# Two attention layers in one kernel: VectorE and ScalarE in a planned order, PSUM banks by turns, scores six units ahead

## The chip, the cores and the metric

One core of a Trainium2 chip. The metric is the device time of the whole kernel in microseconds; lower is better.

## The reference

Two layers over images of 512 channels and 32 x 32 = 1024 tokens, eight images. The first quantises q, k and v to 255 levels with one scale each, taken over all images, and has 8 heads of 64 channels; the second has one head of 512 channels. Both end in a projection that is added to their input.

```python
def _L0_conv_ref(x, gn_w, gn_b, qkv_w, qkv_b, proj_w, proj_b):
    xf = x.reshape(b, c, T)
    h = group_norm(xf, gn_w, gn_b)
    qkv = jnp.einsum('oc,bct->bot', qkv_w, h) + qkv_b[None, :, None]
    q, k, v = jnp.split(qkv.reshape(b * NUM_HEADS, -1, T), 3, axis=1)
    q, k, v = fake_quant(q), fake_quant(k), fake_quant(v)
    w = jnp.einsum('bct,bcs->bts', q * scale, k * scale)
    w = jax.nn.softmax(w, axis=-1)
    a = jnp.einsum('bts,bcs->bct', w, v).reshape(b, c, T)
    return xf + jnp.einsum('oc,bct->bot', proj_w, a) + proj_b[None, :, None]

def _L1_conv_ref(x, gn_w, gn_b, wq, bq, wk, bk, wv, bv, wp, bp):
    t = group_norm(x, gn_w, gn_b).reshape(B, C, H * W).transpose(0, 2, 1)
    q, k, v = (t @ w.T + b for w, b in ((wq, bq), (wk, bk), (wv, bv)))
    attn = jax.nn.softmax(q @ k.transpose(0, 2, 1) / sqrt(C), axis=-1)
    proj = (attn @ v) @ wp.T + bp
    return x + proj.transpose(0, 2, 1).reshape(B, C, H, W)
```

## The kernel before

The kernel runs in four stretches of time.

The first computes q, k and v of layer 0 for all images (tiles `qkps`, `vps`), writes them to DRAM and gathers the extrema for the scales. The second folds the weights of layer 1 (`fold`) while it does layer 0's attention for image 0. The third is the long one: for each image it runs layer 1 (`layer1`) and, between the pieces of it, layer 0's attention for the next image. The fourth is layer 1 of the last image, with nothing between.

Layer 0's attention is cut into units (`attention`): a unit is one block of 128 keys for two heads and 512 queries, 64 units per image. `scores` forms `st` on TensorE, ScalarE takes the exponential into `pt` (L770), and `pt` is split into two halves of 16 bits, `two`: a cast (L777, on ScalarE for even units and on GpSimd for odd ones; on VectorE while the flag `alone` holds, in the second stretch) and a subtraction on VectorE (L778). `weighted` then forms `av` (values) and `sm` (sums over keys). A generator step (`advance`) does four units, a block; scores are formed four units ahead of `weighted`. `finish` copies `av` and `sm` on ScalarE at the end of eight units (L815, L816), sends the sums over DRAM to be inverted, and VectorE divides (L832).

Layer 1 is made of products of matrices, each done as a group of seven products of half size (`seven`): `a_block` (tile `g`), `v_block2` (`v2ps`), `s_block` (`s`, the scores) and `o_run` (`o`), ten groups per image. One group uses two PSUM banks, x and y, into which products are accumulated; between products ScalarE copies a part out (`keep`, tiles `kept_u`, L1055, L1092, L1188), VectorE adds a kept part to a bank (`add`, L1068, L1110, L1125, L1159), and one result is taken whole. In the last image a third bank is used (`third`). A product of g, v2ps or s is four matmuls of 256 columns, one of o eight. `project` is layer 0's last projection (tile `pj`, evicted into `h` at L922), `norm1` the norm of layer 1. In `o_run` the sums over keys (`acc`, L1293) are totalled by TensorE (`sm_l`) and inverted over DRAM (`inverse1`).

TensorE's order is written out by hand: `mm` (L105) ties each matmul to the one before. VectorE and ScalarE have no such tie; the framework's scheduler places their instructions. Pieces that aren't urgent are put into a list (`later`) and taken out one at a time by `chore`, after a count of steps, or all of a name by `settle`. Loads of x1, wp0, wm and h are issued from ScalarE's queue, the others from SP's.

Of the kernel before, what the change touches and what calls it, by code (L numbers as in the profile page):

```python
# [17 lines left out]
P = 128  # L18
# [35 lines left out]
def attn_pair_kernel(  # L54
# [11 lines left out]

    x_v = x.rearrange("b (cc p) h w -> b p cc (h w)", p=P)
# [8 lines left out]
    nc.scalar.dma_start(vec, vecs)  # L76
    ones = const.tile([P, P], F32, name="ones")
    nc.vector.memset(ones, 1.0)
# [10 lines left out]
    nc.vector.memset(gavg, 0.0)  # L89
    with tc.tile_pool(name="band", bufs=1) as band:  # L90
        low = band.tile([P, 32], F32, name="low")
        nc.vector.memset(low[:, 0:GS], 1.0)
        nc.vector.memset(low[:, GS:32], 0.0)
        low_t = band.tile([P, 32], F32, name="low_t")
        nc.vector.transpose(low_t, low)
        for r in range(0, P, 32):
            sq = slice(r, r + 32)
            nc.vector.tensor_tensor(gavg[sq, sq], low[sq, :], low_t[sq, :], ALU.is_equal)
    nc.vector.tensor_scalar(gavg, gavg, 1.0 / GS, None, ALU.mult)
    ident = const.tile([P, P], F32, name="ident")  # L100
    make_identity(nc, ident)
# [3 lines left out]
    def mm(*args, **kw):  # L105
        ins = nc.tensor.matmul(*args, **kw).ins  # L106
# [10 lines left out]
    def aggregate(mv, st, i):  # L117
        nc.vector.bn_aggr(mv[:, i, :], st[:, i, :, :].rearrange("p a s -> p (a s)"))


    def norm_steps(
        src, dst, wcol, bank, nm, ccs=range(CC), fine=False, put=lambda hf, work: work(), mv=None
# [4 lines left out]
        n, c0 = len(ccs), ccs[0]  # L127
        if mv is None:
            st, mv = stat_tiles(n, nm)
            for i, cc in enumerate(ccs):  # L130
                for hf in range(NH):
                    nc.vector.bn_stats(st[:, i, hf, :], src(cc, hf))
# [8 lines left out]
        nc.vector.tensor_sub(d, mv[:, :, 0], ps)  # L141
        mean = small.tile([P, n], F32, tag=f"gmean{n}", name=f"gmean_{nm}")
        nc.vector.tensor_copy(mean, ps)
        nc.vector.tensor_mul(d, d, d)
        nc.vector.tensor_add(d, d, mv[:, :, 1])
# [4 lines left out]
        nc.vector.tensor_scalar(rstd, ps2, EPS, None, ALU.add)  # L150
        nc.gpsimd.tensor_tensor(rstd, rstd, mhalf[:, 0:n], ALU.pow)
        nc.vector.tensor_mul(rstd, rstd, vec[:, wcol + c0 : wcol + c0 + n])
        for hf in range(NH):
            for i, cc in enumerate(ccs):
                put(hf, lambda i=i, cc=cc, hf=hf: nc.vector.tensor_scalar(  # L155
# [27 lines left out]
    with ExitStack() as fast:  # L183
# [50 lines left out]
        def weigh(bank, room, w, wide, nm):  # L234
# [9 lines left out]
            nc.scalar.copy(room, ps)  # L244
# [17 lines left out]
        def widen(dst, col):  # L262
            for e in range(CC):
                nc.vector.tensor_scalar(
# [3 lines left out]
        with tc.tile_pool(name="p1w", bufs=1) as p1w, tc.tile_pool(name="p1", bufs=3) as p1, tc.tile_pool(  # L268
# [15 lines left out]
            def load_folded(tag, ij):  # L284

                two = l1p.tile([P, 2, CC, C], F32, tag=tag, name=f"wn_{tag}")
                for n, i in enumerate(ij):
                    wn[i] = two[:, n]
                    nc.scalar.dma_start(wn[i], w_sq[i])
# [33 lines left out]
            def weight_sums():  # L323
                tt = nc.vector.tensor_tensor
# [28 lines left out]
            def token_sums(b):  # L353
# [4 lines left out]
                tt = nc.vector.tensor_tensor  # L358
# [13 lines left out]
            def add_max(dst, ps, other, mx):  # L372
                nc.vector.tensor_tensor_reduce(
# [1457 lines left out]
```

## Time and profile before

| | us |
|---|---|
| median of 3 runs | 2813.78 (2807.37 to 2815.15) |
| the profiled execution | 2814.92, its span 2813.1 |
| TensorE busy (PE) | 2621.5, 93% |
| VectorE busy (DVE) | 1924.6, 68% |
| ScalarE busy (ACT) | 1152.1, 41% |
| GpSimd busy (POOL) | 280.9, 10% |
| mean granted TensorE clock | 0.990 |

Busy time is the time in which at least one instruction of the engine was under way, and its share is one over the whole span; it has to be read by stretches, which have different limits. In the profile a line such as L106 is a helper's, so tile names tell more than lines. A row of waits names the waiting engine, its tile and line, and after the arrow what released it.

### The profile page before, as it was taken

The numbers are of one execution on the slowest core, as the hardware profiler recorded it, in microseconds if no ns is written. First come the engines' busy times: TensorE is split into PE (matmuls) and PEld (weight loads), VectorE is DVE, ScalarE is ACT, GpSimd is POOL, SyncE is SP. The second block draws the span as 40 slices with busy tenths as digits, with TensorE's granted clock in tenths as the row PEclk, the third lists the DMA queues.
The fourth block names the chain that finished last, engine by engine and source line by source line (L and its number), as shares of the span: only waits on it lengthen the run. The fifth ranks groups of instructions, "written<-read, shape, count | busy, mean of one in ns | idle before, by whom it ended". The sixth has DMA issues, their size and how long they took to land.

```text
span 2813.1 us, 33256 instructions
## 1 busy us (share of the span) xinstructions
PE 2621.5 (93%) x13110; PEld 1650.1 (59%) x13110; DVE 1924.6 (68%) x2772; ACT 1152.1 (41%) x1474; POOL 280.9 (10%) x248
## 2 busy tenths in 40 slices
PE   7999999997779999999999999999999999999998
PEld 3455555552226665665566566656665665567687
DVE  6766665668987767776776677677767766764534
ACT  0011111117955563645465455535563645463021
POOL 0000000000011111111111111111111111110000
PEclk9999999999999999999999999999999999999999
DMA  5233322333321223123212421241233123201401
GB/s 195 101 120 120 113 112 90 120 118 122 106 87 31 72 85 107 54 72 117 76 39 64 128 72 39 85 131 44 73 92 98 52 72 113 71 10 46 142 8 43
DMA packets 147461, 241.94 MB, mean 86 GB/s; under 512 B 26592, under 2 KB 92128, under 8 KB 145760
## 3 DMA queue, kind: packets, MB, share of 16 engines
q1 hardware_dynamic: 116448, 181.50, 19.5%
q10 hardware_dynamic: 30848, 58.23, 6.3%
q8 instruction: 104, 1.70, 0.3%
q14 instruction: 61, 0.50, 0.1%
HBM read 152.86 MB, written 86.28 MB: 85 GB/s over the span
## 4 chain that ended last, share of the span: by engine, by line
PE 50%; DVE 22%; issue 11%; ACT 10%; DMA 5%; POOL 1%; ACTq 0%; SPq 0%; DVEq 0%; POOLq 0%
PE s L106 10%; PE qkps L106 10%; DVE two L778 9%; PE o L106 7%; ACT pt L770 5%; PE pj L106 5%; PE vps L106 5%; PE v2ps L106 4%; PE g L106 4%; ACT two L777 3%; PE av L106 3%; DMA rs<-rs_d 2%; PE st L106 2%; PE sm L106 1%; DVE ao L832 1%
## 5 line engine op out<-in xcount | busy, mean ns | idle before, releaser
L778 DVE TENSOR_TENSOR two<-pt,two 128x1024 f16<-128x1024 f32 x512 | 617.1, 1236 | 254.8 <-ACT two L777 240.4
L770 ACT ACTIVATE pt<-st,esc 128x1024 f32<-128x1024 f32 x512 | 554.7, 1124 | 214.9 <-PE st L106 168.8
L777 POOL CAST two<-pt 128x1024 f16<-128x1024 f32 x218 | 260.9, 1197 | 1537.5 <-ACT pt L770 1531.7
L777 ACT CAST two<-pt 128x1024 f16<-128x1024 f32 x256 | 270.0, 1055 | 1.1
L106 PE MATMUL av<-two,v 128*64 128x512 f16 x2048 | 255.9, 388 | 0.3
L398 ACT ACTIVATE u<-qkps,qkb 128x512 f32<-128x512 f32 x84 | 57.7, 687 | 476.5 <-PE qkps L106 472.1
L106 PE MATMUL s<-g,h 128*128 128x256 f32 x1024 | 238.2, 382 | 13.7 <-DVE p L1125 10.1
L106 PE MATMUL pj<-ao,wp 128*128 128x512 f32 x512 | 223.0, 594 | 0.0
L106 PEld LDWEIGHTS s<-g,h 128*128 128x128 f32 x1024 | 191.7, 190 | 51.1 <-DVE p L1125 16.6
L106 PE MATMUL st<-q,k 64*128 64x512 bf16 x1024 | 166.1, 386 | 56.6 <-ACT pt L770 44.1
L106 PE MATMUL s<-g,sums 128*128 128x256 f32 x768 | 183.7, 386 | 14.3 <-ACT kept_u L1092 14.3
L106 PEld LDWEIGHTS <-v 128*64 128x64 f16 x2048 | 104.5, 110 | 134.4 <-issue 62.5
L106 PE MATMUL o<-p,v 128*128 128x256 f32 x768 | 174.1, 382 | 0.0
L106 PEld LDWEIGHTS s<-g,sums 128*128 128x128 f32 x768 | 142.0, 190 | 50.0 <-ACT kept_u L1092 22.7
L106 PE MATMUL qkps<-x,wqkv 128*128 128x512 f32 x352 | 165.4, 613 | 2.2 <-DVE x L155 2.2
L106 PEld LDWEIGHTS pj<-ao,wp 128*128 128x128 f32 x512 | 96.6, 190 | 119.0 <-issue 115.2
L106 PEld LDWEIGHTS o<-p,v 128*128 128x128 f32 x768 | 144.2, 190 | 27.2 <-issue 8.5
L106 PE MATMUL g<-h,wa 128*128 128x256 f32 x512 | 127.8, 394 | 30.7 <-DVE kept_u L1159 14.4
L106 PE MATMUL qkps<-sums,wa 128*128 128x512 f32 x336 | 153.3, 592 | 0.0
L106 PE MATMUL sm<-two,ones 128*32 128x512 f16 x2048 | 141.2, 387 | 0.0
L106 PEld LDWEIGHTS <-k 64*128 64x128 bf16 x1024 | 35.2, 94 | 174.3 <-issue 173.7
L106 PE MATMUL v2ps<-wm,h 128*128 128x256 f32 x512 | 121.9, 385 | 10.9 <-DVE v L1110 6.6
(218 smaller groups left out, 3530.6 us busy)
## 6 DMA issues: line engine op xcount, KB each, us to landing
rs<-rs_d SPq DMA_DIRECT2D x80, 256.0 KB
x<-in_x_dram SPq DMA_DIRECT2D x32, 512.0 KB
raw<-q_d SPq DMA_DIRECT2D x32, 512.0 KB
raw<-k_d SPq DMA_DIRECT2D x32, 512.0 KB
raw<-v_d SPq DMA_DIRECT2D x32, 512.0 KB
x_d<-h SPq DMA_DIRECT2D x64, 256.0 KB
x<-x_d ACTq DMA_DIRECT2D x64, 256.0 KB
out_dram<-x SPq DMA_DIRECT2D x64, 256.0 KB
```

Source lines behind the costliest of these rows:

```text
L106: ins = nc.tensor.matmul(*args, **kw).ins
L398: nc.scalar.activation(dst, x, AF.Identity, bias=bias)
L770: nc.scalar.activation(pt, st, AF.Exp, scale=esc)
L777: cast(two[:, 0], pt)
L778: nc.vector.tensor_tensor(two[:, 1], pt, two[:, 0], ALU.subtract)
L832: nc.vector.scalar_tensor_tensor(aot, aot, scl[:, 2:3], rs, ALU.mult, ALU.mult)
```

## The change

A recording layer, `InOrder`, stands in front of VectorE and ScalarE. From the third stretch on it ties every instruction of an engine to the one before, as `mm` does for TensorE. It keeps a clock per engine: `mm` advances TensorE's by the number of columns, `do` places an urgent piece with its duration, and `later` lists a piece with its duration, the time from which it can run, and one by which it should. `fill` puts listed pieces ahead of an urgent one as far as they fit before it can begin.

```diff
+    class InOrder:
+        planned = False
+        def __getattr__(self, name):
+            op = getattr(self.engine, name)
+            def call(*args, **kw):
+                ins = op(*args, **kw).ins
+                if InOrder.planned:
+                    if self.last is not None:
+                        tc.add_manual_dep(ins, self.last.name, IN_ORDER, reason="order")
+                    self.last = ins
+            return call
+        def do(self, cost, work, ready=None):
+            if InOrder.planned:
+                ready = pe.t + 0.25 if ready is None else ready
+                self.fill(ready)
+                self.t = max(self.t, ready) + cost
+            work()
+            return self.t
+        def later(self, name, cost, work, ready=0.0, within=30.0):
+            if InOrder.planned:
+                self.chores.append((name, cost, work, max(ready, pe.t), pe.t + within))
+            else:
+                work()
+        def fill(self, limit):
+            if self is dve:
+                act.fill(limit)
+            while True:
+                best, names = None, set()
+                for i, (name, cost, _, ready, due) in enumerate(self.chores):
+                    if name in names:
+                        continue
+                    names.add(name)
+                    begin = max(self.t, ready)
+                    if begin + cost > limit + 0.15:
+                        continue
+                    key = (begin, due)
+                    if best is None or key < best[0]:
+                        best = key, i
+                if best is None:
+                    return
+                self.begin(best[1])
+    dve, act, pe = InOrder(nc.vector), InOrder(nc.scalar), InOrder(nc.tensor)
+    def elements(n):
+        return 0.1 + n * 1.06e-3
+    def awaits(t):
+        pe.t = max(pe.t, t + 0.1)
```

In `mm` `pe.t += math.prod(rhs.shape[1:]) * 1.677e-3 * part` is added. All instructions of VectorE and ScalarE are now issued through `dve` and `act`.

In `attention` all casts that fall into the planned part are ScalarE's, scores are formed six to ten units ahead, and `pt` has four buffers instead of three:

```diff
-        ptp = fast.enter_context(tc.tile_pool(name="ptp", bufs=3))
+        ptp = fast.enter_context(tc.tile_pool(name="ptp", bufs=4))
...
-                cast = nc.scalar.copy
-                if s % 2:
-                    cast = nc.vector.tensor_copy if alone else nc.gpsimd.tensor_copy
...
+                def cast():
+                    at_hand.add(u)
+                    act.copy(two[:, 0], pt)
+                    dve.later("sum", elements(1024), rest, act.t + 0.1, 9.0)
+                if InOrder.planned or s % 2 == 0:
+                    act.later("cast", 1.02, cast, there, 7.0)
+                else:
+                    dve.tensor_copy(two[:, 0], pt)
+                    rest()
...
-                    scores(u + 4)
-                    scores(u + 5)
-                weighted((u, u + 1) if dense else range(u, u + 4))
+                two(scores, u + 6)
...
+                    over_keys(range(u, u + 4))
+                    totals(range(u, u + 4))
+                    two(split, u + 6)
+                    two(scores, u + 8)
+                if s == NT - 4:
+                    finish(b, j, hf)
+                two(split, u + 8)
```

In `seven` the order of the products and of what is taken out changes, and the third bank goes. `free` and `turn` follow the banks in the plan:

```diff
-            product(0, x, True)
-            keep(0, x)
-            product(1, y, True)
-            add(0, y)
-            product(2, x, False)
-            keep(1, x)
-            product(3, y, True)
-            product(4, x, False)
-            keep(2, x)
-            add(2, y)
-            if third is None:
-                product(5, x, False)
-                whole(x)
-            else:
-                z = third(f"{nm}_2").rearrange("p (t n) -> p t n", t=2)
-                product(5, z, True)
-                add(3, z)
-            product(6, y, False)
-            add(1, y)
+            work = (
+                (0, x, True, keep, 0), (1, y, True, add, 0), (2, x, False, keep, 1),
+                (3, y, True, keep, 2), (4, x, False, add, 2), (6, y, False, add, 1),
+                (5, x, False, whole, None),
+            )
+            for i, (n, ps, start, out, m) in enumerate(work):
+                awaits(free[(i + turn) % 2])
+                product(n, ps, start)
+                free[(i + turn) % 2] = out(ps) if m is None else out(m, ps)
+                yield i + 1
```

(The yields of the old form, which number its steps 1 to 7, are left out.) The attention blocks stand elsewhere between the products: before, up to two in one group and none in the next; after, one in each group of `a_block`, `v_block2` and `s_block`, and in `o_run` one after product 0, one after product 3 (around `project` in the second half) and one at the end. There are 16 per image in both.

In `o_run` the sums `t2`, `p12`, `t4` of the probabilities become listed pieces (p2, p3, p4), the inverse of the sums too, and the last result is scaled from its bank at once and stored later; the check of the sums of the last image stands before that:

```diff
             def whole(ps):
-                scale(ps, 1)
-                put(0, 1, ps)
+                settle("o")
+                w = rs[:, 256:512].rearrange("p (o n) -> p o n", o=1)
+                there = dve.do(elements(512), lambda: tt(
+                    *([u[0]] + list(bass.broadcast_tensor_aps(ps, w))), ALU.mult
+                ))
+                dve.later("o", 2 * elements(256), lambda: put(0, 1, u[0]))
+                return there
...
-        alone = False
+        for e in (dve, act):
+            e.t = pe.t
+        InOrder.planned = True
         for n in others():
             dense = n < 0
-            chore(2)
             advance()
```

In `project` the eviction is urgent and the statistics are listed; in `norm1` the first half is urgent and the second listed. The loads of x1, wm, wp0 and h stay on ScalarE's queue, in the fixed order. The unused identity matrix on GpSimd is no longer made.

## The prediction

> **What bounds the kernel now.** The page comes first, then busy time by stage, then TensorE's waits inside one image of the long middle stage, then a few microseconds of its timeline.
>
> ```profile
> PE 2621.5 (93%) x13110; PEld 1650.1 (59%) x13110; DVE 1924.6 (68%) x2772; ACT 1152.1 (41%) x1474; POOL 280.9 (10%) x248
> ...
> 620.00:784.60 164.60, 125.74 (x839) 43.20 (x837) 152.61 (x216) 128.48 (x140) 0.42 (x1) 0.95 0.38 127
> 784.60:843.00 58.40, 46.11 (x232) 18.10 (x228) 45.55 (x57) 29.03 (x32) 11.59 (x9) 0.97 0.26 86
> 843.00:1076.60 233.60, 218.84 (x1273) 145.23 (x1273) 166.41 (x199) 126.00 (x162) 34.60 (x29) 0.99 0.24 73
> 1338.60:1602.00 263.40, 246.62 (x1401) 161.21 (x1397) 186.27 (x233) 135.36 (x173) 39.08 (x33) 0.99 0.26 79
> 2562.00:2805.30 243.30, 238.41 (x1068) 192.35 (x1068) 116.26 (x193) 46.45 (x88) 1.83 (x2) 1.00 0.18 58
> ```
>
> The first line says that TensorE is the bound: 191.6 us of the 2813.1 are left to gain even if no matmul ever waited. The others (window, length, then PE, PEld, DVE, ACT, POOL, clock) say where they lie. Before 620 us the first layer's projections keep TensorE busy 603.6 of 620. From 620 to 784.6 VectorE is the bound (152.6 of 164.6). From 843 to 2562 each image takes about 263.5 us, of which 16.8 are TensorE's idle time; 1719 us hold 6.5 such images, so 110 us. From 2562 on little is idle. The granted clock is 0.97 to 1.00 after 784.6, so it explains none of this.
>
> What TensorE waits for in the image 1338 to 1602:
>
> ```profile
> PE sm_l L106 <- DVE acc L1293: 2.7, 1, 2.7
> PE g L106 <- DVE kept_u L1159: 2.3, 2, 1.7
> PE s L106 <- ACT kept_u L1092: 2.0, 3, 0.7
> PE s L106 <- DVE p L1125: 1.6, 2, 1.3
> PE o L106 <- ACT kept_u L1188: 1.4, 2, 0.8
> PE st L106 <- DVE h L922: 1.3, 2, 1.0
> PE v2ps L106 <- DVE v L1110: 1.3, 2, 1.0
> PE g L106 <- ACT kept_u L1055: 1.0, 1, 1.0
> ...
> 1368.50 1.89 PE L106 MATMUL g<-h,wa 128*128 128x256 f32 x8
> 1371.41 0.67 DVE L1159 TENSOR_TENSOR kept_u<-o,kept_u 128x512 f32<-128x512 f32 x1
> 1372.14 1.99 PE L106 MATMUL g<-h,wa 128*128 128x256 f32 x8 [1.74 <-DVE kept_u L1159]
> ...
> 2756.25 7.07 PE L106 MATMUL s<-g,h 128*128 128x256 f32 x32
> 2763.16 7.07 PE L106 MATMUL s<-g,sums 128*128 128x256 f32 x32
> ```
>
> Columns of the waits are total us, times, longest. There are 14 such rows with 21 waits and 16.5 us in sum; none is large. Nearly all are a bank of PSUM, or a buffer, that VectorE or ScalarE had not yet emptied. The last two lines give the undisturbed pace: four products of 8 matmul records in 6.91 us, 1.727 us each. (A product in o is twice as long, 3.45.) The three lines before them show a wait: from 1368.50 the next two products take until 1373.97, where the next matmuls start, that is 5.47 us against 3.45. So 2.02 us were lost where the row counts 1.74: each wait costs about 0.28 us more than it shows.
>
> **The change part by part.**
>
> *The banks by turns.* Before, products 4 and 5 of a group of seven stand in the same bank, and the third kept part is taken from x after product 4, which both the add and product 6 then wait for. After, it is taken from y after product 3, product 6 goes ahead of product 5, and the built order shows the next group starting in the other bank (7, 6, 7, 6 after a group that ended in 6). Every reader of a bank now has one whole product, 1.727 us, to finish. It needs 0.13 us to start (a product's end to ScalarE's copy in the timeline) and 0.59 (kept_u) or 0.69 (the add). So these rows should go: s 2.0 + 1.6 + 0.5, o 1.4, v2ps 1.3 + 0.7 + 0.5, g 1.0 + 0.5, together 9.5 us per image.
>
> What is late next: ScalarE after an attention block. Its two last exponentials take 2 x 1.12 us behind the block, and every second block two copies of 0.60 stand behind them. Then 2.2 + 1.2 + 0.13 + 0.59 = 4.1 us pass until a short product's bank is free, and TensorE wants it after 2 x 1.727 + 0.1 = 3.55. Of 16 blocks per image 8 lie among short products, 4 of those with the copies: 4 x 0.55 = 2.2 us stay. In the second half three loads of x1 stand on ScalarE's queue ahead of the first kept part of s (issue rows of 0.53 each): 0.9 us. Left 3.1 of 9.5.
>
> *The order of VectorE and ScalarE.* No instruction is added by this; about the same work is put elsewhere. The wait of sm_l (2.7) is the end of a chain of four adds of 0.68. In the new order t2, these adds and one add of the group still have to fit between the exponentials and the second product, but an attention block of 3.9 us now stands ahead of that product in both halves, where before it did in the second only. Counting VectorE's list there gives nothing to wait in the first half and about 2 us in the second: left 2.0. The waits of scores for a projection's eviction and for the norm (1.3 + 0.4 + 0.5) keep one eviction of 0.75 us behind the last product, twice: left 1.2.
>
> At the image's end g waits for the last eviction of o (2.3). After, the last reader of o frees its bank with its first operation, but the stores of wm's four loads move: they were spread (two at 1319.6, one at 1360.5, one at 1364.9) and now stand together on ScalarE behind the two copies and ahead of g's first kept part. The latter comes at 0.4 + 2.2 + 1.2 + 4 x 0.33 = 5.1 us after the block and takes 0.84, where TensorE wants the bank after 3.5: 2.5 left, no gain. The loads themselves (4 x 512 KB) are wanted some 12 us after issue; at the 195 GB/s of the first slice 2 MB take 10.8 us, and the last quarter is wanted four products later, so I cost them nothing.
>
> SP's queue carries the reciprocal's way (rs out, spread back, broadcast): 9.5 us from sm_l's copy at 1216.06 to the first scaling at 1225.53. After, that scaling is wanted two products and a block after sm_l, 10.8 us, in the last image three products, 10.4: hidden, with 1 us to spare; a store ahead of it on SP would cost that.
>
> *The casts leave GpSimd.* 32 casts per image (1.19 us each there) become ScalarE's: 32 x 1.054 = 33.7 us, ScalarE 135 to 169 of 250. They lie beside TensorE as long as they are queued behind evictions, which the plan's order does (kept_u ahead of the casts; in 1134 to 1140 it was behind one). VectorE is to get something back. Where no casts ran on GpSimd (620 to 784.6) against later, the same rows have means of 747 and 1167 ns (k), 747 and 846 (raw), 1279 and 1468 (ao), but 1216 and 1240 for the subtraction `two`. With h (0.54 against 0.69) and x (0.48 against 0.60) the excess is 55 us over 6.75 images, 8 per image. The Trainium skill (SBUF — State Buffer, Who interferes with whom) states that a VectorE instruction with two SBUF inputs and a GpSimd instruction that reads SBUF exclude each other for the whole instruction. By that rule the 32 casts could hold the subtractions up for up to 32 x 1.04 = 33 us per image; the row shows 64 x 0.024 = 1.5. The trace decides: I take 8 us of relief in all. By the rule's upper end VectorE would fall to 153 of 250 rather than 178, and the 2.0 of sm_l would vanish too, 13 us more in all. Either way this counts only where VectorE is last.
>
> *Scores six ahead, a fourth pt buffer.* ScalarE waits for `two` 2.9 us per image; TensorE's own wait for pt is 0.5, which goes. Two more units fall into the stage before the plan starts: VectorE 2 x 1.22 + 0.69 = 3.1 us in the stage that it bounds; against it stands a better lead there, which can give at most VectorE's 12.0 idle us. Neither shows; I take 0, with -6 and +6 as ends.
>
> *The end.* The third bank and the fourth kept part go; the banks by turns cover them. After the last product the check of the sums (some 4.3 us of small operations, by their durations now, with the two wide ones put at 0.68) stands in VectorE's list ahead of the last scaling, which then ends about 8.3 us after product 6 instead of 5.8: +2.5 us.
>
> **The sum.** Left per image 3.1 + 2.0 + 1.2 + 2.5 = 8.8 of 16.5: 7.7 us saved. Some 12 of 21 waits go, 12 x 0.28 = 3.4. That is 11.1 us per image, x 6.5 = 72; less 2.5 at the end: 69.5. The profiled execution took 2814.92 us (span 2813.1), 1.1 above the median of 2813.78: 2744 in terms of the median.
>
> **The rivals.**
>
> *Nearly all waits go* (0.15). The plan knows the engines' durations, so the 8.8 us could be 3, with 18 waits fewer: 13.5 + 18 x 0.28 = 18.5 per image, -120 + 2.5: 2696. For it: VectorE and ScalarE are both at about 70%. Against: the plan gives no time to issues on ScalarE's queue, and TensorE's clock in it doesn't wait for acc.
>
> *The waits only move* (0.07). Sm_l, the image's end and the blocks could take all 16.5 us back, or the order could differ little from the old one where it counts: 2814, within 8.
>
> *ScalarE becomes late* (0.13). It evicts 32 short products per image (8 a, 8 v2ps, 16 s). Behind one cast or exponential an eviction takes 0.13 + 1.05 + 0.59 = 1.77 us, just the 1.727 available; behind two it is 1.1 us late. The waits that go are worth 16.5 + 5.9 = 22 us per image; at 22 / (1.1 + 0.28) = 16 of 32 late evictions all is lost. With all 32 late it is +22 per image, +143 in all; at 24, +11, so 2888. For it: a quarter more work on ScalarE, and evictions next to 16 blocks. Against: the built order has the casts behind the evictions.
>
> *The likeliest case* (0.65) holds 2705 to 2785: residues between 5 and 12 us per image, and -6 to +6 for the early stage.
>
> **How the numbers follow.** The predicted time is 2744. Range 2692 to 2806: it takes in the second case almost wholly and leaves out ScalarE late and half of no change. A measurement here can tell about 0.3%, 8.4 us. Faster by more: 0.65 + 0.15 = 0.80; within: 0.07; slower: 0.13.
>
> **What would show it.** PE busy per image 244 to 246 in a period near 252; no row "st or o waits for kept" inside a group; sm_l and g at the image's end as the largest waits left; POOL near 20 us in all, ScalarE near 1380, VectorE near 1870; k and ao back at 0.75 and 1.28; from the last product to the end 10 us rather than 8. It would be wrong if TensorE waited for ScalarE more than 10 us per image, or if v2ps waited for wm.

## The result, and the profile after

The changed kernel takes 2772.07 us in the median of 4 runs (2760.67 to 2773.30), against 2813.93 for the kernel before (4 runs, 2807.37 to 2815.15). The ratio is 0.9847, 95% interval 0.9817 to 0.9877: 42 us less, clear of the 0.3% that such a measurement can tell. The profiled execution is the fastest of the four: 2760.67 us, span 2758.9, granted clock 0.987; the other three ran at 0.982 and 11 to 13 us longer. Like is compared with like below: profile with profile (54.2 us less), median with median (42 less).

The page's line of busy times:

```profile
PE 2609.1 (95%) x13110; PEld 1659.1 (60%) x13110; DVE 1868.5 (68%) x2768; ACT 1364.7 (49%) x1691; POOL 24.6 (1%) x28
```

Busy time in the early stage, in image 0, in an undisturbed image and in the last one (window, length, PE, PEld, DVE, ACT, POOL, granted clock, DMA):

```profile
620.00:785.60 165.60, 128.31 (x834) 44.37 (x832) 152.93 (x214) 130.43 (x143) 0.42 (x1) 0.91 0.38 125
785.60:1052.90 267.30, 244.49 (x1392) 156.08 (x1388) 175.84 (x222) 172.41 (x211) 1.06 (x1) 0.95 0.20 62
1817.00:2069.80 252.80, 242.78 (x1401) 160.98 (x1397) 178.36 (x232) 166.72 (x206) 1.92 (x1) 1.00 0.26 82
2558.80:2748.80 190.00, 186.54 (x805) 150.77 (x803) 90.28 (x146) 33.00 (x61) 1.01 (x1) 0.99 0.17 52
```

The third window is one image: 252.8 us with 242.8 of TensorE. From here on an image is counted from its first matmul of pj to the next image's. Counted so, the kernel before spends 263.5 us on each of images 1 to 5 in the mean, 17.2 of them with TensorE idle. After, it is 253.9 and 10.1. That is where the gain is: 48 us in images 1 to 5, 5 in image 0, 7 in image 6. The early stage, the last image and the end lost 1.0, 2.5 and 2.3; the 1.0 is no more than the spread of that stage among kernels with the same code there (it ends between 781.7 and 785.6 us).

What TensorE still waits for in the image of the third window (total us, times, longest):

```profile
PE g L190 <- ACT kept_u L81: 3.2, 1, 3.2
PE sm_l L190 <- DVE acc L81: 2.2, 1, 2.2
PE s L190 <- ACT kept_u L81: 1.4, 2, 1.2
PE st L190 <- DVE h L81: 1.1, 2, 0.6
PE g L190 <- DVE kept_u L81: 1.1, 1, 1.1
```

These five rows are 9.0 of 9.8 us; before, fourteen rows made 16.5. The rows for p, v and o's kept parts are gone. The few that are left are longer, and the longest stands at the image's end. The chain to it, as the timeline of image 1 shows it (start, duration, engine, operation; idle time before it in brackets):

```profile
1100.79 1.92 DVE L81 TENSOR_SCALAR h<-h,gmean_b,grstd_b 128x512 f32<-128x512 f32 x4
...
1108.19 2.35 DVE L81 TENSOR_TENSOR two<-pt,two 128x1024 f16<-128x1024 f32 x2
1108.33 1.99 PE L190 MATMUL g<-h,wa 128*128 128x256 f32 x8 [1.07 <-DVE kept_u L81]
1109.50 2.25 ACT L81 ACTIVATE pt<-st,esc 128x1024 f32<-128x1024 f32 x2 [5.59 <-DVE two L81]
...
1112.69 0.84 ACT L81 ACTIVATE kept_u<-g,gb 128x256 f32<-128x256 f32 x2
...
1113.58 2.53 PE L190 MATMUL g<-sums,wa 128*128 128x256 f32 x8 [3.26 <-ACT kept_u L81]
1115.90 3.09 PE L190 MATMUL g<-h,wa 128*128 128x256 f32 x8
```

Read it backwards. TensorE waits 3.26 us for the kept part. ScalarE takes that late because its exponentials stood still for 5.59 us: all pt buffers were full, and the subtraction that frees one (`two`) stood in VectorE's fixed order behind the norm, the sums and the closing operations of o. The last two lines show something else: after the wait two products take 2.32 and 2.93 us from start to start, where 1.73 is the pace. The granted clock is at half speed there.

### The profile page after: what moved, and what is told of

It is laid out like the page before. It is cut to its first block, busy times and chain, and to the rows that moved or that the text cites. A ratio compares the mean times of both kernels' runs of the same rounds, so it can differ in the third digit from the quotient of the medians.

```text
span 2758.9 us, 33247 instructions
## 1 busy us (share of the span) xinstructions
PE 2609.1 (95%) x13110; PEld 1659.1 (60%) x13110; DVE 1868.5 (68%) x2768; ACT 1364.7 (49%) x1691; POOL 24.6 (1%) x28
## 4 chain that ended last, share of the span: by engine, by line
PE 73%; DVE 15%; ACT 5%; issue 2%; DMA 2%; ACTq 1%; POOL 1%; SPq 0%; DVEq 0%
PE qkps L190 12%; PE s L190 12%; PE o L190 11%; PE v2ps L190 7%; PE av L190 6%; PE vps L190 6%; PE g L190 6%; PE pj L190 5%; DVE two L81 5%; PE st L190 4%; PE sm L190 3%; ACT pt L81 2%; ACT two L81 1%; DVE h L81 1%; DVE sums L81 1%
## 5 line engine op out<-in xcount | busy, mean ns | idle before, releaser
L81 ACT ACTIVATE pt<-st,esc 128x1024 f32<-128x1024 f32 x512 | 547.1, 1115 | 403.1 <-PE st L190 279.2
L81 DVE TENSOR_TENSOR two<-pt,two 128x1024 f16<-128x1024 f32 x512 | 607.0, 1215 | 87.1 <-ACT two L81 87.0
L81 ACT CAST two<-pt 128x1024 f16<-128x1024 f32 x473 | 478.6, 1052 | 27.1 <-issue 19.2
L81 DVE TENSOR_TENSOR p<-s,kept_u 128x512 f32<-128x512 f32 x90 | 62.1, 691 | 116.1 <-PE s L190 97.1
L190 PE MATMUL o<-g,vsum 128*128 128x256 f32 x512 | 120.1, 388 | 0.0
```

Of the source, the lines that this page charges most:

```text
L81: ins = op(*args, **kw).ins
L190: ins = nc.tensor.matmul(ps, lhsT=lhsT, rhs=rhs, **kw).ins
```

## The experiments

Two theories stood at the start. A, the prediction's: the banks by turns carry the gain (6.4 of 7.7 us of waits per image). B: the fixed order of VectorE and ScalarE carries it. "Idle" is TensorE's, and it and the period are means over images 1 to 5 of the profiled run. Each kernel ran beside the kernel before on the same chip. "Profiled" is the time of the execution that the profile shows.

| kernel | median us | profiled us | ratio to before, 95% interval | clock of the runs | period | idle |
|---|---|---|---|---|---|---|
| before | 2813.9 | 2814.9 | | 0.987 to 0.990 | 263.5 | 17.2 |
| after | 2772.1 | 2760.7 | 0.985 (0.982 to 0.988) | 0.982 to 0.987 | 253.9 | 10.1 |
| a_oldbanks | 2786.7 | 2787.0 | 0.990 (0.988 to 0.992) | 0.984 to 0.987 | 257.1 | 12.0 |
| b_banks | 2823.0 | 2826.7 | 1.003 (1.002 to 1.004) | 0.979 to 0.985 | 267.0 | 17.7 |
| b_banks2 | 2792.2 | 2794.5 | 0.991 (0.990 to 0.993) | 0.987 to 0.990 | 262.5 | 15.2 |
| b_six | 2839.8 | 2841.2 | 1.008 (1.006 to 1.010) | 0.982 to 0.984 | 268.6 | 21.5 |
| a_four | 2850.9 | 2852.6 | 1.011 (1.008 to 1.015) | 0.965 to 0.972 | 269.5 | 17.8 |
| a_free | 2748.5 | 2747.3 | 0.977 (0.975 to 0.978) | 0.991 to 0.994 | 254.3 | 9.1 |
| a_pool | 2752.0 | 2749.8 | 0.978 (0.976 to 0.980) | 0.985 to 0.988 | 252.3 | 8.6 |
| f_pool | 2766.1 | 2765.2 | 0.982 (0.980 to 0.984) | 0.990 to 0.993 | 257.3 | 12.8 |
| a_waits | 2785.3 | 2785.7 | 0.989 (0.987 to 0.991) | 0.982 to 0.985 | 260.3 | 12.8 |
| t_two | 2735.5 | 2737.1 | 0.971 (0.969 to 0.973) | 0.987 to 0.990 | 251.6 | 7.7 |
| p_best | 2747.5 | 2746.6 | 0.976 (0.973 to 0.978) | 0.990 to 0.993 | 253.0 | 8.8 |
| t_best | 2713.7 | 2714.2 | 0.965 (0.963 to 0.966) | 0.993 to 0.995 | 249.5 | 6.7 |

The changed kernel's median lies 11 us above its profiled run, at a lower clock; in every other kernel the two agree within 4 us. So what an experiment gains or loses against the changed kernel depends by 11 us on which of the two is taken. The text gives the median's difference first and the profile's beside it; periods and waits are the profiles'.

### The banks, undone and alone

a_oldbanks: the old sequence in the new kernel.

```diff
-                (3, y, True, keep, 2), (4, x, False, add, 2), (6, y, False, add, 1),
-                (5, x, False, whole, None),
+                (y, True, ()), (x, False, ((keep, 2, x), (add, 2, y))),
+                (x, False, ((whole, None, x),)), (y, False, ((add, 1, y),)),
```

> The changed kernel with the seven products of a group put back into the old banks and the old sequence (products 4 and 5 in one bank, the third kept part taken from x after product 4, the last two products swapped back); the plan, its fixed order and the casts stay. Theory A (the prediction's: the banks by turns save about 6.4 us of waits per image and some 9 restarts of 0.28, so 9 of the 11 us per image): slower than the changed kernel by 9 x 6.5 = 58 us, back near 2830, with rows of s, o, v2ps and g waiting for kept_u and for p of about 9 us per image again. Theory B (the fixed order along the plan carries the gain, since a plan that knows the durations also gets the old banks empty in time): slower by less than 15 us, 2775 to 2787. Halfway, 2800, would say that each is worth the same.

It is 14.6 us slower than the changed kernel, just inside theory B's size; profile with profile it is 26.4, above B's 15 and far below A's 58. In its image from 1570.8 on:

```profile
PE s L190 <- ACT kept_u L81: 4.3, 4, 1.7
PE g L190 <- ACT kept_u L81: 4.0, 2, 3.1
```

The waits for kept parts do come back (s 1.4 to 4.3, o 0 to 1.2, v2ps 0 to 0.7), but the wait of sm_l goes in exchange, so the idle time is only 1.9 us per image more, and the period 3.2.

b_banks: the new sequence in the kernel before, with the four operations that follow g moved behind its last product.

```diff
+                work = (
+                    (0, x, True, keep, 0), (1, y, True, add, 0), (2, x, False, keep, 1),
+                    (3, y, True, keep, 2), (4, x, False, add, 2), (6, y, False, add, 1),
+                    (5, x, False, whole, None),
+                )
```

> The kernel before with one thing of the change: the products of a group take the two banks strictly by turns (where no third bank is used); the order of VectorE and ScalarE is still the scheduler's, the casts stay on GpSimd, scores stay four ahead. Theory A: the bank's reader gets a whole product of 1.727 us however the other engines are ordered, so 35 to 58 us faster than before, 2756 to 2780. Theory B: without the fixed order the evictions still stand behind casts and exponentials, so less than 15 us faster, above 2798.

It is 8 us slower than the kernel before. The largest row of its waits in the image from 1588.5 on:

```profile
PE g L106 <- DVE x L1184: 6.1, 2, 3.7
```

Its place in the timeline:

```profile
1645.01 0.86 DVE L1184 SCALAR_TENSOR_TENSOR x<-o,ob,x 128x256 f32<-128x256 f32 x2
...
1645.93 3.35 PE L106 MATMUL g<-h,wa 128*128 128x256 f32 x8 [3.66 <-DVE x L1184]
```

The rows that the turns were to take away fell, by 5.3 us per image in the mean (theory D below counts 5.6), though new ones of o for p and v2ps for g came up with 0.9 and 1.1. Then a third new row took 6.1 back: the product taken whole now comes last, and in the old code three operations of VectorE read its bank before g may have it. And with these waits came spells of half clock: one followed each of the six waits of 3.7 us and five of the seven shorter ones. In all 19 spells lie between 785 us and the last product, where the kernel before has 6.

b_banks2 frees that bank with the first operation, as the change does.

```diff
-                scale(ps, 1)
-                put(0, 1, ps)
+                tt(*([u[0]] + list(bass.broadcast_tensor_aps(ps, w))), ALU.mult)
+                put(0, 1, u[0])
```

> The kernel before with the banks by turns, as in b_banks, and one thing more from the change: the product of o that is taken whole is scaled from its bank into the first kept part, and the two sums with x read that, so the bank is free after 0.69 us instead of after the scaling and both sums. Theory D (in b_banks the turns did take 5.6 us of waits per image away, and gave 6.1 back at the image's end, where g waited for that bank twice): the row 'g for x' goes, TensorE idle per image falls from 17.3 to 11 to 12, and the half-speed spells that followed those waits go too: 2755 to 2785, so half or more of the gain without plan, cast move or fixed order. Theory B (without the plan other waits come up in their place): 2800 to 2825.

The row went and the time fell by 31 us, to 2792, 7 above theory D's range. Idle is 15.2, not 11 to 12, since st for h and g for kept_u grew to 3.0 and 2.9. So the banks with the freed bank are worth 23 us on the kernel before, and the turns 15 to 26 in the changed one: neither A's 58 nor nothing.

### Six ahead, undone and alone

a_four:

```diff
-            for u in (0, 2, 4):
+            for u in (0, 2):
...
-                two(scores, u + 6)
+                two(scores, u + 4)
```

> The changed kernel with scores four units ahead instead of six; the fourth pt buffer, plan, order, banks and casts stay. The prediction counted this part at nothing (-6 to +6 in the early stage, 0.5 us per image of waits for pt): 2766 to 2780. Rival E (six ahead is what gives the casts and subtractions their room, now that all casts are on ScalarE): 20 to 60 us slower, with waits for two or pt of 2 us or more in every image; on the other side image 0's start, where the blocks stand back to back, could be shorter by some us.

It is 79 us slower than the changed kernel (92 by the profiles), beyond rival E's 60 and slower even than the kernel before. In the image from 1597.5 on:

```profile
PE av L190 <- DVE two L81: 10.3, 8, 6.3
PE av L190 <- ACT two L81: 5.7, 3, 2.1
```

In no other kernel do these rows reach 1 us in the whole third stretch. The longest wait of them stands at the image's end:

```profile
1637.89 2.94 ACT L81 CAST two<-pt 128x1024 f16<-128x1024 f32 x3
...
1652.87 2.35 DVE L81 TENSOR_TENSOR two<-pt,two 128x1024 f16<-128x1024 f32 x2
1654.14 1.77 PE L190 MATMUL av<-two,v 128*64 128x512 f16 x6 [6.27 <-DVE two L81]
```

There the casts had ended at 1640.83. It was VectorE that was late: the subtractions stood in its fixed order behind the norm's scalings and sums and the closing operations of o. The other 9.7 us lie inside the image, and the longest of these, 2.1 us, are waits for ScalarE's cast. So rival E's reading holds, but not for the casts alone: with all casts on ScalarE, and casts and subtractions placed by the plan, four units are too few. The part that the prediction counted at nothing is the one without which the change would have lost.

b_six gives the same lead to b_banks2, with the splits made after the products that they follow in the change.

```diff
-        ptp = fast.enter_context(tc.tile_pool(name="ptp", bufs=3))
+        ptp = fast.enter_context(tc.tile_pool(name="ptp", bufs=4))
...
+                split = [scores(v) for v in (u + 6, u + 7) if v < len(units)]
                 weighted((u, u + 1) if dense else range(u, u + 4))
+                for f in split:
+                    f()
```

> The kernel before with the banks by turns and the free bank of b_banks2, and scores six units ahead with a fourth pt buffer as in the change (its unused constant of 512 B per partition dropped for the room); still no plan, no fixed order, casts on GpSimd. Theory H (six ahead is needed only because the change moved the casts to ScalarE and plans them late; with the casts on GpSimd TensorE never waited for two): 2780 to 2797, within 10 us of b_banks2's 2792. Rival E (the deeper lead itself is worth what a_four lost, 7 us per image): 2735 to 2760, so the plan would add nothing.

Both theories missed: it is 48 us slower than b_banks2. Idle rose from 15.2 to 21.5. Two of its waits in the image from 1595.9 on (the first was 0.9, the second not there):

```profile
PE s L103 <- DVE p L1138: 3.9, 3, 2.9
PE pj L103 <- DVE h L920: 2.4, 1, 2.4
```

So rival E falls here: under the scheduler's order the lead, with the splits moved as they are, is worth nothing. Why it costs so much was not followed further. The pair shows that plan and lead work together: in these forms each without the other is slower than the kernel before. It does not show what in the planned kernel needs the lead, the casts on ScalarE or the order: four units ahead with a_pool's casts was not run.

### The fixed order and the casts, undone

a_free leaves out the ties; the operations are still issued in the plan's sequence.

```diff
                 if InOrder.planned:
-                    if self.last is not None:
-                        tc.add_manual_dep(ins, self.last.name, IN_ORDER, reason="order")
                     self.last = ins
```

> The changed kernel without the ties that fix the order of VectorE and ScalarE: the same operations are issued along the same plan, but the scheduler puts them into its own order on each engine. Theory A: within 15 us of the changed kernel (2765 to 2787), with TensorE's waits per image up by 1 to 2 us. Theory B: most of the gain goes, 2795 to 2830, with kept_u late behind casts on ScalarE (waits of g, s, v2ps and o for ACT kept_u of more than 8 us per image).

Neither: it is 24 us faster than the changed kernel, 13 by the profiles. The period is the same (254.3 against 253.9). The profiles differ in image 0 (259.5 us against 267.3), at the end (7.1 against 10.1, the check of the sums having slid into earlier idle time) and in the early stage (162.1 against 165.6, at a granted clock of 0.95 against 0.91). The early stage lies ahead of all ties, so its 3.5 us are not theirs; and the rest of the 24 goes with the clocks of the runs, 0.991 to 0.994 against 0.982 to 0.987. Theory B falls: nothing is lost without the tie, and some 11 us are gained in image 0 and at the end. What the plan's sequence of issue is worth by itself no run shows.

a_pool:

```diff
+                if InOrder.planned and s % 2:
+                    at_hand.add(u)
+                    nc.gpsimd.tensor_copy(two[:, 0], pt)
+                    dve.later("sum", elements(1024), rest, there + 1.3, 9.0)
```

> The changed kernel with every second cast of the planned stage back on GpSimd. Theory A (the relief of VectorE is 8 us per image and lies beside TensorE, but each of these casts now comes 0.2 us later to its subtraction): 0 to 10 us slower, VectorE near 186 us per image instead of 178, ScalarE near 135, k near 1.17 us and ao near 1.47 in the mean, the subtraction within 0.03 us of 1.216. Rival by the Trainium skill's rule (SBUF — State Buffer, Who interferes with whom: a two-input VectorE instruction and a GpSimd instruction that reads SBUF exclude each other): subtractions up to 1 us longer, VectorE at 200 or more per image, and 13 us or more per image in waits, 2850 or above. Rival C (ScalarE's load is what costs now): faster by 5 to 15 us, since 34 us per image of ScalarE's time are freed ahead of the first kept parts.

It is 20 us faster, a little more than rival C asked, and 11 by the profiles. VectorE stands at 186.5 us per image instead of 178.3, so the relief of 8 us was read rightly in sum. It does not lie where it was expected: k and ao rose to 0.89 and 1.30 us in the mean, not to 1.17 and 1.47. The subtraction's mean is 1213 ns against 1215. One meeting of a subtraction and a cast shows why:

```profile
842.20 3.49 DVE L81 TENSOR_TENSOR two<-pt,two 128x1024 f16<-128x1024 f32 x3
844.71 1.87 POOL L873 CAST two<-pt 128x1024 f16<-128x1024 f32 x1 [7.23 <-ACT pt L81]
```

A cast with nothing on VectorE beside it takes 1.04 us. Here it takes 1.87 and ends 0.9 us after the subtractions. Only 20 of the 217 casts in the trace overlap a subtraction; in all 20 the subtraction had begun first and took its usual 1.21 to 1.23 us, and the cast ended 0.90 us after it. So the two do exclude each other, as the rule of the rival says, but here they seldom meet, and when they do it is GpSimd that waits. With 30 us per image less work on ScalarE the kernel is faster although VectorE has 8 more, so it was ScalarE's time that counted.

f_pool does both.

> The changed kernel without the ties and with every second cast back on GpSimd: two undoings together that alone gave 2748 and 2752. If they take away different waits: 2772 - 24 - 20 = 2728, TensorE idle near 7.6 us per image. If both take away the same one (ScalarE's first kept part late behind casts and issues at the image's end): 2743 to 2750, idle 8.4 to 9.

They do not add: 2766, slower than either alone and than the 2743 to 2750 of the cautious reading, and by the profiles 5 us slower than the changed kernel. Idle is 12.8, with rows of s for g, s for p and pj for h of 2.7, 1.8 and 1.9 us in the image from 1815.8 on. Without the ties the scheduler fills VectorE's order in its own way, and the waits land elsewhere.

### The largest waits left

a_waits takes four of them at what seemed their causes.

```diff
-                act.dma_start(t, src)
+                nc.sync.dma_start(t, src)
...
-                elif step == 2:
-                    settle("p2")
-                    settle("acc")
-                    rs = inverse1(b, hf, acc)
-                    rs_there = pe.t + 9.5
-                elif step == 3:
-                    settle("p3")
+                elif step == 2:
+                    settle("p2")
+                elif step == 3:
+                    settle("p3")
+                    settle("acc")
+                    rs = inverse1(b, hf, acc)
+                    rs_there = pe.t + 9.5
...
                     need(u - 4)
+                    if InOrder.planned and u - 3 not in at_hand:
+                        i = next((i for i, c in enumerate(act.chores) if c[0] == "cast"), None)
+                        if i is not None:
+                            act.begin(i)
...
                     settle("p4")
                     finish(2)
+                    if final and hf == NH - 1:
+                        settle("o")
+                        check_sums()
```

> The changed kernel with the largest waits that are left taken away at their cause: wm's four loads issued from SP instead of ScalarE (wait of g for ScalarE's kept_u, 3.3 us per image); the row sums of o one product later (sm_l, 2.3 us per image); a cast put ahead of each exponential in the order (the chain of 3.4 us per unit at image 0's start, 14.8 us of waits for pt); the check of the sums one product earlier (10.1 us from the last product to the end). If each cause is the right one: 5.6 x 6 + about 8 + 3 = 45 us of waits, and with them the half-speed spells of the clock that follow waits of 2 us and more, 5 to 15: 2712 to 2727. Rival F (the waits only move to what comes next on ScalarE and VectorE): 2750 to 2772. By row it is told apart in any case: which of the four rows goes and which new one stands in its place.

It is 13 us slower than the changed kernel (25 by the profiles). Sm_l went, and image 0 fell from 267.3 to 255.1. Two rows of the image from 1558.8 on:

```profile
PE g L190 <- ACT kept_u L81: 5.0, 2, 4.0
PE pj L190 <- DVE h L81: 3.2, 1, 3.2
```

The first rose with wm's issues gone from ScalarE, so they were not its cause; one of the edits even lengthened it, since a cast of 1.03 us now stood between the two exponentials ahead of the kept part. The second is new (3.7 us in the mean of images 1 to 5). The end did not move (10.7): after the fifth product too, the check stood ahead of the last additions. SP's own waits show why pj waits, first in a_waits from 2070 to 2092:

```profile
SPq L1107 <- DMA rs_d<-rcs: 4.7, 1, 4.7
```

The same in the changed kernel from 2060 to 2078:

```profile
SPq L1103 <- DMA rs_d<-rcs: 1.1, 1, 1.1
```

Half of wm's loads, two of 512 KB, now left SP just ahead of the small store of the reciprocals, for whose landing SP then waited 4.7 us instead of 1.1. The first scaling waited for it on VectorE, and pj's eviction stood behind that scaling.

t_two tests the chain that the timeline of after shows, and leaves wm alone.

```diff
         nc.gpsimd.tensor_tensor(rstd, rstd, mhalf[:, 0:n], ALU.pow)
+        if InOrder.planned:
+            act.settle("cast")
+            dve.settle("sum")
...
             def whole(ps):
-                settle("o")
+                while sum(c[0] == "o" for c in dve.chores) > 2:
+                    dve.begin(next(i for i, c in enumerate(dve.chores) if c[0] == "o"))
...
                     finish(1)
-                    settle("o")
```

> The changed kernel with two edits in VectorE's order at the image's end: the pending subtractions that free the pt buffers come ahead of the norm's scalings (in the time that VectorE waits for GpSimd's power), and the last product of o is scaled ahead of the last sums with x. wm's loads stay on ScalarE's queue. Theory G (g waits 3.3 us per image for ScalarE's first kept part because ScalarE's exponentials wait 5.6 us for a pt buffer that VectorE frees behind 16 operations; the four issues cost nothing): the row g for ACT kept_u falls to 0.5 us or less, g for DVE kept_u stays between 1 and 2.5, TensorE idle near 7 to 8 us per image, half-speed spells at 60 us into each image gone: 2740 to 2755. Rival (the prediction's: the wait is wm's issues ahead of the kept part): the row stays at 2.5 or more and the time at 2765 to 2775.

2735.5, 37 us faster than the changed kernel (24 by the profiles) and below the range of theory G. Its timeline at the same place, a few images on:

```profile
2097.04 3.48 DVE L81 TENSOR_TENSOR two<-pt,two 128x1024 f16<-128x1024 f32 x3
...
2102.09 1.92 DVE L81 TENSOR_SCALAR h<-h,gmean_b,grstd_b 128x512 f32<-128x512 f32 x4
...
2103.73 1.11 ACT L81 ACTIVATE pt<-st,esc 128x1024 f32<-128x1024 f32 x1 [1.24 <-PE st L190]
...
2110.16 1.99 PE L190 MATMUL g<-sums,wa 128*128 128x256 f32 x8 [0.85 <-ACT kept_u L81]
```

The subtractions now come ahead of the norm's scalings. The exponentials that waited 5.59 us for VectorE wait 1.24 for their scores, and the wait for ScalarE's kept part is 0.85 us instead of 3.26, with wm's issues where they were. Theory G holds in its cause, and the prediction's reading of that wait falls. The row fell to 0.9, not to the 0.5 that G named: ScalarE's copy now waits 2.45 us for VectorE's sums with x. The two edits were made together; how much the second gave was not separated.

p_best joins a_pool, the cast ahead of each exponential, t_two's edits and a check of the sums at the very end.

> All that helped by its row, together: the changed kernel with every second cast on GpSimd, a cast ahead of each exponential, t_two's two edits, and the check of the sums behind the last scaling; the fixed order stays. From a_pool's 2752: image 0 shorter by 6 to 10 us, the waits of g 2 to 4 us per image less with their half-speed spells, the end 3 us shorter: 2710 to 2730. If the edits only trade one wait for another, as in f_pool: 2745 to 2765.

2747.5: of the two outcomes named, the trade. Idle is 8.8, not better than a_pool's 8.6. G's wait for ScalarE's kept part is 2.6 us per image again, in spite of t_two's edits; why was not followed. The end is 12.0 us: behind the last scaling the check's chain itself sets it.

t_best keeps t_two and adds the later row sums without the move of wm, the extra cast for image 0's start alone, and the check of the sums after the fourth product instead of the sixth.

```diff
+                elif step in (2, 3):
+                    settle(f"p{step}")
+                    if step == 2 + (not final):
+                        settle("acc")
+                        rs = inverse1(b, hf, acc)
+                        rs_there = pe.t + 9.5
                 elif step == 4:
+                    if final and hf == NH - 1:
+                        settle("o")
+                        check_sums()
...
+                    if InOrder.planned and u < 100 and u - 3 not in at_hand:
```

> t_two (2735) with three more edits: the row sums of o one product later in all images but the last (the row sm_l for acc, 2.3 us and a half-speed spell of 3.4 us near 239 us into each image); a cast ahead of each exponential at image 0's start only; the check of the sums three products earlier, in the time that VectorE idles in the last group of o. wm's loads stay on ScalarE. Expected by row: sm_l gone, 2.3 + 0.3 + 1.7 us in each of 7 images = 25 to 30; image 0's start 4 to 7; the end 10 to 7: 2697 to 2710. Rival (in a_waits it was the later row sums, not wm's loads on SP's queue, that let the first scaling hold VectorE up and pj wait 3.7 us for h): pj for h at 2 us or more again, and 2730 to 2745.

2713.7, ratio 0.9645 (0.9626 to 0.9664), 4 us above the range and 16 below the rival's. Busy times of one image:

```profile
1783.10:2032.70 249.60, 242.80 (x1400) 160.51 (x1396) 178.08 (x232) 166.46 (x205) 1.92 (x1) 1.00 0.26 83
```

One of its waits there (the longest row is 1.8 us in two times, and g for ScalarE's kept part is 0.8):

```profile
PE pj L190 <- DVE h L81: 0.9, 1, 0.9
```

Sm_l is gone and pj for h is 0.9 (0.7 in the mean), against 3.7 in a_waits. So there it was chiefly wm on SP, unless t_two's edits, which t_best has and a_waits has not, play a part in it. Image 0 is 251.1 us, the end 7.0, and no half-speed spell is left in images 1 to 6. This version beats both kernels: it is 98 us below the kernel before on the same chip, and 58 below the changed one (46 by the profiles).

## Why the prediction was right, and where it was not

The sum. In the terms of the profile it said 2814.92 - 69.5 = 2745.4 and 2760.7 was measured; the median is 28 above the forecast and inside the range. Per image the forecast was 7.7 us of waits and 3.4 of restarts. Measured in images 1 to 5: 7.1 less idle, and 2.6 less of busy TensorE, 0.4 of that the clock. So 9.7 against 11.1. The other 2.2 us, over 11.8 waits fewer per image, make 0.19 us a wait; the prediction took 0.28 from a single one.

What it said would be seen was nearly all seen: TensorE busy 243.7 of 253.9 us in the mean (244 to 246 in a period near 252 was said), no st or o waiting for a kept part inside a group, sm_l and g at the image's end as the largest rows, POOL 24.6, ScalarE 1364.7, VectorE 1868.5, k and ao at 752 and 1281 ns, 10.1 us to the end. All these signs were right while several of the causes behind them were not. They told the state, not the cause. That the time fell inside the range is in part luck: the range is 114 us wide, and parts that were counted at nothing turned out worth 79 us one way (six ahead) and about 20 the other (the casts; the ties).

*Banks by turns.* Of the nine rows named six went, v2ps for g fell to 0.2 and s for kept_u to 1.4, together 1.6 where 3.1 was forecast; the ninth, g for ScalarE's kept_u, is the image's end below. So the list of waits was right. The step that failed is the credit: 6.4 us of waits per image were put down to the banks alone. Undone, they cost 1.9 of idle; alone, they gained nothing until the whole product's bank was freed too. The other 5.2 of the 7.1 us stand with the plan, the lead and the new places of the attention blocks together. No run takes these apart, and the blocks' places were never put back, so the cause of that share stays open. The prediction saw that o's last reader "frees its bank with its first operation" and didn't count it as a part with a price.

*The order.* Sm_l was put at 2.0 left and was 2.2, st 1.2 and 1.1. The rows were well sized. That the tie could cost more than it gives (a_free: 24 us in the median, some 11 of it in the places that the ties reach) was not considered.

*The image's end.* "2.5 left" was close to the 3.2 measured, for the wrong reason. The sum of 5.1 us had wm's issues, 4 x 0.33, in the kept part's way. In the timeline two copies and the kept part follow each other without a gap while the issues go out beside them. What was late were the exponentials, for want of a pt buffer. Reading which engine idles before the waited-for operation would have shown the direction: not the queue ahead of it, but what its own producer waits for.

*The casts.* The relief of 8 us was right (8.2 in a_pool). By the rule of the Trainium skill (SBUF — State Buffer, Who interferes with whom) it could have been up to 33; the rule holds where the two meet in a_pool, but few meet, and the subtraction came first. Costing the move itself at nothing was not right: undoing it gains 20 us (11 by the profiles), where the prediction's rival of a late ScalarE put its loss at 74 and came from short products, not from the image's end.

*Six ahead.* "Neither shows; I take 0, with -6 and +6" is the step most wrong in size: 79 us in the planned kernel. The prediction weighed it in the early stage alone, where the trace had waits to show, and not against the casts and subtractions that the same change places later.

*Image 0's start and the end.* The start was in that same term: 14.8 us of waits for pt in image 0 against 5.5 before (where g waited for h once instead, 7.2), a chain of exponential, cast and subtraction of 3.4 us per unit. The fixed order makes part of it: without the ties (a_free) 9.3 us of these waits are left. The end was sized rightly: +2.5 forecast, +2.3 measured.

*The clock* was said to explain nothing of the time before, and the forecast left it as it was. Span times what is missing in the granted clock gives 34 us before (0.988), 50 in the median of the changed kernel (0.982), 16 in t_best (0.994). So some 16 us of the 28 by which the median missed lie there, and 34 of t_best's 58. In the profiles 13 us of the changed kernel's 37 lie in image 0, where the waits for pt stand, and 5 of 28 before. Why three of the four runs had 0.982 and the profiled one 0.987 was not settled; no trace of the three was kept.

## What to carry to other kernels

Parts of a change that lose one by one can gain together: cost each with the others in place, above all a lead or a buffer count when the operations that it feeds are moved. A wait is explained only when the chain is followed to what its releaser itself waited for; here the queue in front of it was innocent, and moving that queue made things worse. A fixed order puts every later operation behind an early one's buffer or transfer, so the operations that free a buffer belong ahead of those that merely have time.

## What the runs showed of the hardware

*A long wait of TensorE is paid twice.* In the 14 profiles, after the first pj, waits of 0.5 us and more were matched with the spells of half clock that began during them or up to 2.5 us behind. Of 667 waits below 1.5 us 7% had one, of 91 from 1.5 to 2 us 22%, of 96 from 2 to 3 us 54%, of 64 of 3 us and more 86%. Spells are multiples of 3.4 us, and each such stretch loses 1.7. Many of these waits are one wait that recurs in every image, so the shares are rough. The edits fit them: g's wait of 3.3 us near 60 us into an image had a spell in two of images 1 to 6 of the changed kernel; in a_waits, where it is 4.0, it had one in all six, and in t_two, where it is 0.9, in none. Sm_l's wait of 2.2 to 2.6 near 239 us had one in four of its five images in t_two; in t_best both are gone. So a wait makes a spell likely, not certain. The Trainium skill (TensorE: Matmul & The Clock Gate, HAM oscillation — how this bites in real kernels) sets the rule that gaps of more than about 3.4 us are to be avoided; by it the 2.2 us of sm_l would be free of this. Here waits of 2 to 3 us had a spell in more than half of the cases, so the measurement decides. By these shares few long waits are worse than the same time in many short ones, and a change that leaves fewer waits can still lose more to the clock.

*DMA issues on ScalarE's queue cost its engine no time that shows here.* In image 1 of the changed kernel wm's four issues, some 0.43 us each, went out between 1110.8 and 1112.6, while an exponential, the copies of 0.58 and 0.60 us and the kept part ran back to back.
